# Gate's and up's shared low-rank products together in two folds of the second phase of an fp32 attention and expert-FFN layer

## The chip, the cores and the metric

The kernel runs on one core of a Trainium2 chip. The metric is the device time of one execution in microseconds, the median of several runs. Everything is float32.

## The reference, cut to what matters

```python
xn = layernorm(x)                                   # x: 2 x 1024 tokens, 512 wide
x + attention(xn) + ffn(xn)
# attention: Q, K = elu(.) + 1 of the projections, 16 heads of 32
#   out = (Q @ (K^T V)) / (Q . sum(K) + 1e-8);  out @ wo.T + bo
# ffn (DFF 1376, 8 experts, top 2, rank 8)
gate = x @ W_gate + (x @ sA_gate @ sB_gate) * scale + expert_lora(x, A_gate, B_gate, w)
up   = x @ W_up   + (x @ sA_up   @ sB_up)   * scale + expert_lora(x, A_up,   B_up,   w)
hidden = silu(gate) * up
out  = hidden @ W_down + (hidden @ sA_down @ sB_down) * scale + expert_lora(hidden, ...)
```

The terms with `sA` and `sB` are shared by all tokens. So the kernel adds the product `sA @ sB * scale` to the weights themselves, once, before it uses them. This is called a *fold*. Gate and up each have one: for ten blocks of 128 columns of DFF, taken in pairs `j` and `j + 5` (`NP` is 5), and for the last 96 columns, the *rest*.

## The kernel before, in words

One program works through four phases. The order of the instructions on TensorE (PE), VectorE (DVE), ScalarE (ACT) and GpSimd (POOL) is the order in which the Python code issues them. The transfers on SyncE's queue (SP) are put in order by the scheduler of the language when the program is built. An engine takes its instructions strictly in order, so one that waits holds all behind it.

*Phase one* (to about 178 us) normalises and transposes x, projects the keys, and builds for each of two batches of 1024 tokens the matrix K^T V Wo. The object `Finish` does this last part; for the second batch its products take PSUM banks in turn from four tags `pg0` to `pg3` (`Finish.bank`, L502 to L507). Its last four products (`pko`, L553) are copied out by ACT (L554), and `query_unit(0)` runs around them. Then the pool of eight equal banks `ps` is opened (L996), which hands out banks in rotation. Its first users are the five products `psa` of `shared_factors` (L560): they bring the shared factor sA into `sat`, with rows 0 to 7 of each group of 32 partitions holding one 128-column piece.

*Phase two* (178 to 243 us) computes the queries of the second batch in `query_unit(1, ...)`, a row of products named P2, P1, P6, P5, P7, P3, P4 with hooks between them, then the low-rank inputs `low_rank_in` (L851), the denominators (L873), and the rest columns of gate and up in `rest(0)` and `rest(1)` (L1074 to L1094), which call `between[0]` and `between[1]` after their two halves. Folds in this phase:

- `fold_rest(i)`, with `i` 0 for gate and 1 for up: four matmuls with 8 rows each, one for each piece of 128 rows of the weights, into four banks of their own (L1046), then eight additions on DVE (L1049). Gate's stands in hook P7, up's stands after P4 and `load_last`.
- `fold(0, i)`: `fold_pe` has four such matmuls of 256 columns into four banks (L958), `fold_adds` four additions on DVE (L967), `fold_sums` four sums of weight blocks on DVE (L971 to L974) that the fast 2x2 block products need. Gate's stands in `rest(0)`, up's in `rest(1)`; each bank of 512 columns is half used.

`rest(1)`'s second `between` forms the inner weight sums for products 1, 5 and 6 (L1176 to L1179) on DVE. In between, `attend(1, g)` multiplies the queries with the reciprocal denominators that PE spreads into `pb` (L895, L903), `token_diffs(1, ...)` runs on POOL (L1005), and `token_sums_1` on DVE (L1154 to L1157). After `rest(1)` POOL forms more weight and token sums (L1176 to L1179, L1132, L1154 to L1157).

`load_weights(j, late)` loads the weights of a pair. With `late` it first writes one element of each target on DVE (`hold`, L147), so that the transfer can't start before DVE has come to that place. Pair 0 is loaded so, pair 1 is not.

*Phase three* (243 to about 451 us) has ten units, `unit(j, b)`, with gate and up of one pair for one batch: two levels of 2x2 block products (L1202 and L1262), and low-rank products (L1257). The folds of the pairs 1 to 4 stand in its hooks (`next_pair`). A unit adds its products on DVE (L1284 and others). *Phase four* multiplies the hidden features and the attention with their output weights.

Of the kernel before, what the change touches and what calls it, by code (L numbers as in the profile page):

```python
# [15 lines left out]
P = 128  # L16
# [21 lines left out]
def layer_kernel(  # L38
# [23 lines left out]
    nc = tc.nc  # L62
# [10 lines left out]
    RANK = LR // (E + 1)  # L73
# [4 lines left out]
    NC = D // P  # L78
# [163 lines left out]
    def bank(name, shape=None, tag=None):  # L242
        tag = tag or (next(tags) if tags else "ps")
        return ps_pool[0].tile(shape or [P, TB], F32, tag=tag, name=name)
# [250 lines left out]
    class Finish:  # L495


        def __init__(self, b, pg, ksum):
            self.b, self.pg, self.ksum = b, pg, ksum
            self.made = 0  # L500

        def bank(self, name, shape=None):  # L502
            if self.b == 0:
# [195 lines left out]
    def load_weights(t, w):  # L699
        hold(t[:, 0, 0:1])  # L700
        nc.sync.dma_start(out=t, in_=by_chunk(w))
# [185 lines left out]
    def attend(b, g=None):  # L887

        if b:
            todo = [(c, g) for c in range(NC)]  # L890
            by = []
            for c in range(NC):
                rows = slice(c * 32, (c + 1) * 32)
                by.append(bank(f"pb{b}_{g}_{c}"))
                nc.tensor.matmul(by[c], spread[rows, g, :], dens[b][rows, :], start=True, stop=True)  # L895
        else:
            k = len(attended)
            attended.extend((k, k + 1))
            todo = [(i % NC, i // NC) for i in attended[-2:]]
            by = [bcs[i] for i in attended[-2:]]  # L900
        for (c, g), t in zip(todo, by):
            v = qt[b, c, g]
            nc.vector.tensor_mul(v, v, t)  # L903
            if b == 0:
                spread_den()

            j, i = c % NPQ, c // NPQ
            nc.sync.dma_start(
                out=q_dram[b][j][:, :, 2 * i + g, :].rearrange("s p n -> p s n"),
                in_=v.rearrange("p (s n) -> p s n", n=UT),  # L910
            )
# [35 lines left out]
                )  # L947
        wsum[j] = (ws, sb)

    def fold_pe(j, i, tags=()):  # L950

        sb = wsum[j][1]
        pf = []
        for k in range(NC):
            rows = slice(k * 32, k * 32 + RANK)
            name = f"pf{i}_{j}_{k}"
            pf.append(spare_bank(tags[k], name) if tags else bank(name))
            nc.tensor.matmul(pf[k][:, 0 : 2 * P], sat[rows, i, :], sb[rows, i, :, :], start=True, stop=True)  # L958
        return pf

    def fold_adds(j, i, pf):

        t = wsum[j][0][i]
        v = t.rearrange("p s (k m) -> p s k m", m=P)
        for k in range(NC):
            at = v[:, k // 2 : k // 2 + 7 : 6, k % 2, :]
            nc.vector.tensor_add(at, at, pf[k][:, 0 : 2 * P].rearrange("p (h m) -> p h m", h=2))  # L967

    def fold_sums(j, i):
        t = wsum[j][0][i]  # L970
        nc.vector.tensor_add(t[:, S1, :], t[:, A21, :], t[:, A22, :])  # L971
        nc.vector.tensor_sub(t[:, S3, :], t[:, A11, :], t[:, A21, :])
        nc.vector.tensor_sub(t[:, S2, :], t[:, S1, :], t[:, A11, :])
        nc.vector.tensor_sub(t[:, S4, :], t[:, A12, :], t[:, S2, :])  # L974
# [28 lines left out]
    def token_diffs(b, tag):  # L1003
        xdiff.append(ffn.tile([P, TB], F32, tag=tag, name=f"xdiff{b}"))
        nc.gpsimd.tensor_sub(xdiff[b], xa[b][:, 0:TB], xa[b][:, TB:BT])  # L1005

    def fold(j, i):
        def f():
            fold_adds(j, i, fold_pe(j, i))
            fold_sums(j, i)  # L1010

        return f

    RA = P // 2
# [2 lines left out]
    def rest_cols(i):  # L1019

        return slice(i * RA, (i + 1) * RA), slice(P + i * RB, P + (i + 1) * RB)
# [15 lines left out]
                nc.sync.dma_start(out=sb[k * 32 : k * 32 + RANK, i, :], in_=bw[ER:LR, RC])  # L1037
        return t, sb, bd

    def fold_rest(i):  # L1040
        t, sb, _ = w_rest
        pf = []
        for k in range(NC):
            rows = slice(k * 32, k * 32 + RANK)
            pf.append(bank(f"pfr{i}_{k}"))
            nc.tensor.matmul(pf[k][:, 0:REST], sat[rows, i, :], sb[rows, i, :], start=True, stop=True)  # L1046
        for k in range(NC):
            for at, f in zip(rest_cols(i), (slice(0, RA), slice(RA, REST))):
                nc.vector.tensor_add(t[:, k, at], t[:, k, at], pf[k][:, f])  # L1049

    def rest(b, between=(None, None)):
        t, _, bd = w_rest
        spare = [f"qt{k}{g}" for k in range(NC) for g in range(2)]
        blk = [ts(g, TB) for g in range(2)]

        def gated_rows(ps, first, n, g, dst):

            h, v = (
                p2w.tile([P, TB], F32, tag=spare.pop(0), name=f"{n_}{b}_{g}_{dst.start}", bufs=1) for n_ in ("hr", "ur")
            )  # L1060
            gr, ur = slice(first, first + n), slice(first + n, first + 2 * n)
            nc.scalar.activation(h[gr, :], ps[gr, :], AF.Silu)
            nc.scalar.copy(v[gr, :], ps[ur, :])

            def rest_of():
                nc.vector.tensor_mul(h[gr, :], h[gr, :], v[gr, :])
                nc.sync.dma_start(
                    out=r_dram[b][:, dst, g, :].rearrange("s p n -> p s n"),
                    in_=h[gr, :].rearrange("p (s n) -> p s n", n=UT),
                )  # L1070

            later(rest_of)

        ps = bank(f"pr{b}_2")  # L1074
        halves = [ps[2 * RB * g : 2 * RB * (g + 1), :] for g in range(2)]
        for g in range(2):
            nc.tensor.matmul(halves[g], bd[:, P:], xa[b][:, blk[g]], start=True, stop=False, skip_group_check=True)
        for k in range(NC):
            for g in range(2):
                nc.tensor.matmul(  # L1080
                    halves[g], t[:, k, P:], xt(b, k, blk[g]), start=False, stop=(k == NC - 1), skip_group_check=True
                )
        flush()
        for g in range(2):
            gated_rows(ps, 2 * RB * g, RB, g, slice(RA, REST))
        for g in range(2):
            ps = bank(f"pr{b}_{g}")
            nc.tensor.matmul(ps, bd[:, 0:P], xa[b][:, blk[g]], start=True, stop=False)
            for k in range(NC):
                nc.tensor.matmul(ps, t[:, k, 0:P], xt(b, k, blk[g]), start=False, stop=(k == NC - 1))  # L1090
            flush()
            gated_rows(ps, 0, RA, g, slice(0, RA))
            if between[g]:
                between[g]()  # L1094
# [5 lines left out]
    for _ in range(2):  # L1100
# [1 line left out]
    token_diffs(0, "xd")  # L1102
    query_unit(1, {
        "P5": [lambda: attend(0)],
        "P7": [lambda: fold_rest(0), lambda: attend(0)],
        "P3": [lambda: attend(0)],
        "P4": [lambda: attend(0), lambda: load_weights(0, True)],
    })
    load_weights(1)
    def u_tile(name):  # L1110
        return up_.tile([P, TB], F32, tag="u", name=name)

# [37 lines left out]
    def token_sums_1(eng, b):  # L1150

        t = xnT[b][0][:, :, TB:BT].rearrange("p k (h n) -> p k h n", n=TH)
        b11, b21 = tsum[b][1][:, 0], tsum[b][1][:, 1]
        eng.tensor_sub(t[:, 0, 0], b11[:, TH:], b11[:, 0:TH])  # L1154
        eng.tensor_sub(t[:, 0, 1], b21[:, TH:], t[:, 0, 0])
        eng.tensor_sub(t[:, 1, 0], b21[:, TH:], b11[:, TH:])
        eng.tensor_sub(t[:, 1, 1], b21[:, 0:TH], t[:, 0, 1])  # L1157
        inner_tokens(b, (1,), lambda i, k: t[:, k // 2, k % 2])
# [309 lines left out]
        return sb, wdr, bd, *diffs  # L1468

    sb_d, wdr, bd_sb, wdr_diff, bd_diff = load_last()  # L1470
    fold_rest(1)
    low_rank_in(2)
    low_rank_in(3)
    denominators(1)
    list(token_sums_56(nc.vector, 0, slot(6, [2, 4, TH], "ti56_0")))
    rest(0, (fold(0, 0), lambda: attend(1, 0)))
    attend(1, 1)
    token_diffs(1, "den")
    token_sums_1(nc.vector, 0)
    rest(1, (fold(0, 1), lambda: list(inner_weight_sums(nc.vector, 0, (1, 5, 6)))))  # L1480
    flush()
    ps8.close()
    p2_stack.close()
# [37 lines left out]
    def next_pair(j):  # L1521

        pf = {}


        def pe(i):
            return lambda: pf.update({i: fold_pe(j, i, FREE[i])})

        def adds(i):
            return lambda: fold_adds(j, i, pf.pop(i))  # L1530

        def sums(eng, *ps):
            return lambda: list(inner_weight_sums(eng, j, ps))

        last = {}

        def last_sums(n):
            def f():
                g = last.setdefault(0, inner_weight_sums(nc.vector, j, (1, 5, 6)))
                for _ in range(n):  # L1540
                    next(g, None)

            return f

        return (
            {"6c": [pe(0)], "1d": [adds(0)], "6d": [pe(1)], "7": [adds(1)]},
            {"6c": [lambda: fold_sums(j, 0)], "2c": [lambda: fold_sums(j, 1), sums(nc.gpsimd, 3)],
             "3b": [sums(nc.gpsimd, 2), last_sums(2)], "3d": [last_sums(3)]},
        )
# [572 lines left out]
```

## Time and profile before

| what | value |
|---|---|
| runs | 728.38, 729.91 and 730.34 us; median 729.91 us |
| the profiled execution's own time | 730.1 us |
| its span, first to last instruction | 728.3 us |
| mean granted clock of TensorE | 0.999 |
| PE busy | 717.8 us of the span |
| DVE busy | 579.8 us |
| ACT busy, POOL busy | 198.1 us, 143.4 us |
| PE busy from 168 to 182 us | 13.66 of 14 us |
| PE busy from 182 to 243 us | 61.00 of 61 us |
| PE busy from 243 to 304 us | 60.16 of 61 us |

In the profile a matmul in float32 has two records for each instruction: a product that is one line of the code counts twice. "x8" behind a group of the four fold matmuls is four matmuls. Durations of matmuls overlap with those of their neighbours, since they are pipelined; the chain of work, whose pieces follow each other without overlap, gives the time that a group takes from its neighbours.

### The profile page before, as it was taken

How to read it: one execution, taken by the hardware profiler on the slowest of the kernel's cores; microseconds unless marked ns; L12 is line 12 of the kernel's file. 1: busy time of each engine (PE TensorE's matmuls, PEld its weight loads, DVE VectorE, ACT ScalarE, POOL GpSimd, SP SyncE). 2: the span in 40 equal slices, each digit the busy share in tenths (PEclk: the TensorE clock that was granted, in tenths of full speed). 3: DMA queues.
4: the chain of work that ended last, by engine and by line, in shares of the span. 5: the costliest groups of instructions: out<-in, count | busy, mean ns of one | idle time of the engine just before them, and what ended most of it. 6: DMA issues, size and time to landing. Idle time of an engine off the chain costs nothing.

```text
span 728.3 us, 9908 instructions
## 1 busy us (share of the span) xinstructions
PE 717.8 (99%) x3428; PEld 493.1 (68%) x3428; DVE 579.8 (80%) x1330; ACT 198.1 (27%) x438; POOL 143.4 (20%) x176
## 2 busy tenths in 40 slices
PE   8999999999999999999999999999999999999997
PEld 6666676454433566666667667566688899899896
DVE  5788767777587588878878878878988789998874
ACT  3533412454443233333333333333200000000000
POOL 4014011101000770310310310544520100000000
PEclk9999999999999999999999999999999999999999
DMA  4253000313575101211201201333662444523101
GB/s 155 85 157 106 11 1 1 97 32 112 158 212 154 26 5 58 87 32 59 88 29 59 87 30 59 116 126 134 202 195 101 134 158 132 158 87 109 59 16 44
DMA packets 61734, 66.85 MB, mean 92 GB/s; under 512 B 10866, under 2 KB 49522, under 8 KB 61428
## 3 DMA queue, kind: packets, MB, share of 16 engines
q1 hardware_dynamic: 61154, 66.20, 29.0%
q8 instruction: 27, 0.44, 0.3%
q14 instruction: 23, 0.19, 0.1%
q10 hardware_dynamic: 530, 0.02, 0.0%
HBM read 44.11 MB, written 22.09 MB: 91 GB/s over the span
## 4 chain that ended last, share of the span: by engine, by line
PE 83%; DVE 12%; ACT 3%; issue 1%; DMA 0%; DVEq 0%; ACTq 0%
PE ab L1202 16%; PE b L1262 8%; PE po L1899 7%; PE pg L401 5%; PE pya L1771 4%; PE pxa L1771 3%; PE pqu L772 3%; PE pyb L1771 3%; PE ph L1639 3%; PE x L1202 3%; PE pxb L1771 2%; PE pyc L1771 2%; PE pxa L851 2%; PE b L1257 2%; PE pr L1090 2%; PE pye L1771 2%
## 5 line engine op out<-in xcount | busy, mean ns | idle before, releaser
L1262 PE MATMUL b<-t,w 128*128 128x512 f32 x160 | 83.2, 601 | 0.7 <-DVE t L1284 0.7
L401 PE MATMUL pg<-kt,xn 128*128 128x512 f32 x128 | 58.7, 594 | 0.5 <-DVE kt L345 0.5
L1284 POOL TENSOR_TENSOR r<-r,r 128x512 f32<-128x512 f32 x20 | 30.1, 1524 | 84.5 <-DVE t L1284 82.9
L1202 PE MATMUL ab<-ti,wi 128*128 128x256 f32 x180 | 45.4, 379 | 0.0
L1202 PEld LDWEIGHTS ab<-ti,w 128*128 128x128 f32 x140 | 25.1, 189 | 29.4 <-DVE r L1230 8.2
L1284 DVE TENSOR_TENSOR r<-r,r 128x512 f32<-128x512 f32 x60 | 44.9, 788 | 0.0
L1202 PEld LDWEIGHTS ab<-ti,wi 128*128 128x128 f32 x180 | 34.2, 190 | 13.2 <-issue 5.0
L1202 PE MATMUL ab<-ti,w 128*128 128x256 f32 x140 | 41.2, 387 | 0.5 <-DVE r L1230 0.2
L401 PEld LDWEIGHTS pg<-kt,xn 128*128 128x128 f32 x128 | 23.2, 190 | 22.6 <-issue 20.6
L1235 ACT COPY r<-ab 128x256 f32<-128x256 f32 x50 | 18.6, 372 | 71.1 <-PE ab L1202 71.1
L1230 DVE TENSOR_TENSOR r<-r,ab 128x256 f32<-128x256 f32 x50 | 20.8, 417 | 20.2 <-ACT r L1227 19.7
L1262 PEld LDWEIGHTS b<-t,w 128*128 128x128 f32 x160 | 29.2, 190 | 11.3 <-issue 5.9
L1238 DVE TENSOR_TENSOR r<-r,ab 128x256 f32<-128x256 f32 x50 | 20.8, 417 | 15.9 <-ACT r L1235 15.7
L1212 ACT COPY r<-ab 128x256 f32<-128x256 f32 x50 | 18.6, 373 | 48.5 <-PE ab L1202 47.0
L1899 PE MATMUL po<-wd,f 128*128 128x256 f32 x140 | 30.9, 380 | 0.1
L410 POOL TENSOR_TENSOR ksum<-ksum,kt 128x512 f32<-128x512 f32 x12 | 15.8, 1319 | 71.7 <-DVE lg L447 42.3
L1223 ACT COPY r<-ab 128x256 f32<-128x256 f32 x50 | 18.6, 372 | 40.8 <-PE ab L1202 40.8
L1899 PEld LDWEIGHTS po<-wd,f 128*128 128x128 f32 x140 | 26.4, 190 | 4.4 <-issue 0.5
L1202 PE MATMUL ab<-xnT,w 128*128 128x256 f32 x100 | 29.4, 390 | 0.0
L1842 DVE TENSOR_TENSOR f<-f 128x256 f32<-128x256 f32 x84 | 29.3, 416 | 0.1
L1202 PE MATMUL ab<-xnT,wi 128*128 128x256 f32 x100 | 28.1, 379 | 0.0
L1202 PEld LDWEIGHTS ab<-xnT,w 128*128 128x128 f32 x100 | 18.1, 189 | 10.8 <-issue 4.5
(450 smaller groups left out, 1655.7 us busy)
## 6 DMA issues: line engine op xcount, KB each, us to landing
h_dram<-h SPq DMA_DIRECT2D x40, 256.0 KB
f<-h_dram SPq DMA_DIRECT2D x10, 512.0 KB
x_ring<-in_x_dram SPq DMA_DIRECT2D x16, 256.0 KB
q_dram<-qt SPq DMA_DIRECT2D x16, 256.0 KB
xr<-in_x_dram SPq DMA_DIRECT2D x16, 256.0 KB
out_dram<-xr SPq DMA_DIRECT2D x15, 256.0 KB
w<-in_w_up_dram SPq DMA_DIRECT2D x10, 256.0 KB
w<-in_w_gate_dram SPq DMA_DIRECT2D x10, 256.0 KB
```

What stands on the lines that cost most here:

```text
L401: nc.tensor.matmul(pg[m], xns[n][:, ts(m, P)], kt, start=(j == 0), stop=(j == TPBATCH - 1))
L772: nc.tensor.matmul(banks[c], wqs[p][:, k, ts(c, P)], tsum[b][p][:, k, :], start=(start and k == 0), stop=(k == 1), skip_group_check=True,)
L1202: nc.tensor.matmul(out, w, t, start=start, stop=True, skip_group_check=True)
L1212: nc.scalar.copy(self.r[0][:, H0], self.ua)
L1230: nc.vector.tensor_add(self.r[1][:, H1], self.r[1][:, H1], self.lo)
L1238: nc.vector.tensor_add(self.r[1][:, H0], self.r[1][:, H0], self.lo)
L1262: nc.tensor.matmul(pb[m], ws[m][:, A_OF[p], ts(k, P)], tsum[b][p][:, k, :], start=start, stop=True, skip_group_check=True)
L1284: eng.tensor_add(to[m], t[m], v[m])
L1639: nc.tensor.matmul(phs[u][g * ER : (g + 1) * ER, :], a, f[:, g, :], start=(ns[0] == 0 and n == 0), stop=(last and n == len(chunks) - 1), s ...
L1771: nc.tensor.matmul(o, lhsT, rhs, start=first, stop=True, skip_group_check=True)
L1842: op(t[:, at, :], t[:, x_, :], t[:, y, :])
L1899: nc.tensor.matmul(ps[p][:, q, :], lhsT, rhs, start=start, stop=stop, skip_group_check=True)
```

## The change

- `Finish.made` starts at 3 instead of 0: the banks of the second batch's products shift by one tag. The products `pc`, `pr`, `pv`, `pw0`, `pw1` and the four `pko` stood on pg0, 1, 2, 3, 0 and 1, 2, 3, 0; they stand on pg3, 0, 1, 2, 3 and 0, 1, 2, 3.
- `fold_pe` takes a list of parts `ms`. With both parts, gate's four matmuls write the first halves of four banks, and up's four matmuls the second halves. In phase two both are done in `rest(0)`; DVE adds all eight there (`first_fold`). The eight sums of both parts stand after `token_diffs(1, ...)`. `rest(1)`'s first `between` is now the inner weight sums, its second is empty. In phase three the folds stay apart, up's writing the second half of its banks.
- `fold_rest` is called once, where up's was: eight matmuls into four banks, and eight additions, each over gate and up together. The call in hook P7 is gone.
- Pair 1 is loaded with `late`, which adds four small writes on DVE.

```diff
@@ class Finish
-            self.made = 0
+            self.made = NC - 1
@@
-    def fold_pe(j, i, tags=()):
+    def fold_pe(j, tags=(), ms=(0, 1)):
...
         for k in range(NC):
-            rows = slice(k * 32, k * 32 + RANK)
-            name = f"pf{i}_{j}_{k}"
+            name = f"pf{ms[0]}_{j}_{k}"
             pf.append(spare_bank(tags[k], name) if tags else bank(name))
-            nc.tensor.matmul(pf[k][:, 0 : 2 * P], sat[rows, i, :], sb[rows, i, :, :], start=True, stop=True)
+        for i in ms:
+            for k in range(NC):
+                rows = slice(k * 32, k * 32 + RANK)
+                nc.tensor.matmul(pf[k][:, ts(i, 2 * P)], sat[rows, i, :], sb[rows, i, :, :], start=True, stop=True)
         return pf
@@ def fold_adds
-            nc.vector.tensor_add(at, at, pf[k][:, 0 : 2 * P].rearrange("p (h m) -> p h m", h=2))
+            nc.vector.tensor_add(at, at, pf[k][:, ts(i, 2 * P)].rearrange("p (h m) -> p h m", h=2))
@@
-    def fold_rest(i):
+    def fold_rest():
         t, sb, _ = w_rest
-        pf = []
+        pf = [bank(f"pfr{k}", [P, 2, REST]) for k in range(NC)]
+        for i in range(2):
+            for k in range(NC):
+                rows = slice(k * 32, k * 32 + RANK)
+                nc.tensor.matmul(pf[k][:, i, :], sat[rows, i, :], sb[rows, i, :], start=True, stop=True)
         for k in range(NC):
-            rows = slice(k * 32, k * 32 + RANK)
-            pf.append(bank(f"pfr{i}_{k}"))
-            nc.tensor.matmul(pf[k][:, 0:REST], sat[rows, i, :], sb[rows, i, :], start=True, stop=True)
-        for k in range(NC):
-            for at, f in zip(rest_cols(i), (slice(0, RA), slice(RA, REST))):
-                nc.vector.tensor_add(t[:, k, at], t[:, k, at], pf[k][:, f])
+            for at, f in ((slice(0, P), slice(0, RA)), (slice(P, None), slice(RA, REST))):
+                v = t[:, k, at].rearrange("p (i n) -> p i n", i=2)
+                nc.vector.tensor_add(v, v, pf[k][:, :, f])
@@
-        "P7": [lambda: fold_rest(0), lambda: attend(0)],
+        "P7": [lambda: attend(0)],
...
-    load_weights(1)
+    load_weights(1, True)
@@
-    fold_rest(1)
+    fold_rest()
...
-    rest(0, (fold(0, 0), lambda: attend(1, 0)))
+
+    def first_fold():
+        pf = fold_pe(0)
+        for i in range(2):
+            fold_adds(0, i, pf)
+
+    rest(0, (first_fold, lambda: attend(1, 0)))
     attend(1, 1)
     token_diffs(1, "den")
+    for i in range(2):
+        fold_sums(0, i)
     token_sums_1(nc.vector, 0)
-    rest(1, (fold(0, 1), lambda: list(inner_weight_sums(nc.vector, 0, (1, 5, 6)))))
+    rest(1, (lambda: list(inner_weight_sums(nc.vector, 0, (1, 5, 6))), None))
@@ def next_pair
-            return lambda: pf.update({i: fold_pe(j, i, FREE[i])})
+            return lambda: pf.update({i: fold_pe(j, FREE[i], (i,))})
```

In the built program the counts on PE, ACT and POOL are as before; DVE has eight additions less and four small writes more. On SP's queue four things move: the two loads of up's pair 1, which stood before the first `bc` loads, and those of gate's pair 1 now all follow the loads of pair 0; the small loads for the last phase (`wdr`, `bd_sb`) stand earlier; and the eight small loads `sb2` stand before the eight stores `q_dram1` of `attend(1, ...)` instead of after them.

More of the change, by code (lines that the diff above doesn't have):

```diff
@@ L1005, in token_diffs @@
         nc.gpsimd.tensor_sub(xdiff[b], xa[b][:, 0:TB], xa[b][:, TB:BT])
[L1007 to L1012, printed above, removed]
     RA = P // 2
```

## The prediction

> **What bounds the kernel now.** I read the page first: its busy times, and the shares of the chain of work that ended last.
>
> ```profile
> PE 717.8 (99%) x3428; PEld 493.1 (68%) x3428; DVE 579.8 (80%) x1330; ACT 198.1 (27%) x438; POOL 143.4 (20%) x176
> PE 83%; DVE 12%; ACT 3%; issue 1%; DMA 0%; DVEq 0%; ACTq 0%
> ```
>
> PE is busy for nearly the whole span, and most of the chain is PE's. So what is to be gained is PE time, or one of PE's few waits. The list of waits of PE, asked from 165 to 262 us, where the change lies, has two lines (total us, times, longest):
>
> ```profile
> PE b L1262 <- DVE t L1284: 0.7, 1, 0.7
> PE psa L560 <- ACT gt L554: 0.3, 1, 0.3
> ```
>
> All else in this stretch is PE after PE. The chain of waits shows what the folds take from their neighbours (start, us, what):
>
> ```profile
> 168.34 1.38 PE psa L560 x10
> ...
> 195.81 0.41 PE pfr L1046 x8
> 196.22 3.63 PE pqu L772 x8
> 199.85 3.43 PE pqv L772 x8
> 203.28 0.41 PE pfr L1046 x8
> ...
> 221.54 0.64 PE pf L958 x8
> 222.18 1.06 PE pr L1088 x2
> ...
> 238.01 0.64 PE pf L958 x8
> 238.66 1.06 PE pr L1088 x2
> ```
>
> Eight records of 512 columns take 3.43 us, but 3.63 behind `pfr`; two take 1.06 behind `pf` where 3.43 / 4 = 0.86 is due. So each group of fold matmuls costs its own piece and a restart of 0.20 us in the next. DVE's and POOL's timelines show the rest (start, us, engine, what):
>
> ```profile
> 222.20 1.41 DVE L967 TENSOR_TENSOR w<-w,pf 128x256 f32<-128x256 f32 x4 [1.26 <-PE pf L958]
> ...
> 227.76 4.87 DVE L903 TENSOR_TENSOR qt<-qt,pb 128x512 f32<-128x512 f32 x8 [1.96 <-PE pb L895]
> ...
> 242.19 0.80 DVE L1176 TENSOR_TENSOR wi<-w 128x384 f32<-128x384 f32 x1
> ...
> 256.52 3.35 DVE L1284 TENSOR_TENSOR r<-r,r 128x512 f32<-128x512 f32 x2
> ```
>
> ```profile
> 241.75 0.83 POOL L1176 TENSOR_TENSOR w<-w 128x128 f32<-128x128 f32 x1 [11.31 <-DVE w L974]
> ...
> 257.60 1.72 POOL L1132 TENSOR_TENSOR ti<-t 128x512 f32<-128x512 f32 x1
> ```
>
> DVE has idle time around the folds. POOL starts its sums when the last fold sum is done (L974). The two additions at 256.52 take 3.35 us, where two of this size otherwise take 1.28; they delay the addition that PE waits for at 260.12.
>
> **What the Trainium skill says.** "TensorEngine Tiling (Array Packing)", Key Properties: a change of the tiling mode drains TensorE. The trace agrees: the restart of 0.20 us stands at each change between the 8-row matmuls and full ones. "TensorE: Matmul & The Clock Gate", The mechanism: a weight load runs beside matmuls only where its row group differs. The trace fits: the four row groups run together, so that a group is two waves (a record per row group each), and a wave takes 0.64 / 2 = 0.32 us where 256 columns stream in 0.43 / 2 = 0.21. "SBUF — State Buffer", Who interferes with whom: a DVE instruction with two SBUF inputs and a GpSimd instruction that reads SBUF block each other. The trace agrees: 1.7 us instead of 0.64 at 256.52, beside POOL.
>
> **The change part by part.**
>
> *Shifted banks.* The list of waits has `psa` (bank of pg0) waiting for ACT's copy of `pko`. Before, the last of four copies stood in that bank; now the first does. The four copies take 2.04 us from 166.25 (ACT's timeline), so the first is done by 166.8, and PE comes at 168.0. The idle 0.35 us before `psa` goes, and its first record no longer lasts 377 ns against 275 of the others (`psa`'s instructions): 0.35 to 0.45 us, taken as 0.40. Next late is the bank of the fifth `psa`, which DVE reads from 168.03 to 168.72 (L831); PE gets there at about 168.0 + 8 × 0.11 = 168.9. The bank of the fourth copy now goes to `pxa`, which starts at 169.2; that copy ends at 168.29. Both ends: 0 if another wait takes its place, 0.5.
>
> *`fold_rest` once.* Gone in P7: 0.41 + 0.20 = 0.61 us. Added after P4: two waves, at most another 0.41 us, at least the streaming of 2 × 96 columns, 0.16. Saved 0.20 to 0.45 on PE; I take 0.20, since the same row groups need their weights again. On DVE, P7 loses 1.00 us. After P4 eight additions of 128 and 64 columns replace eight of 64 and 32. From 0.125 us (8 in 1.00, 48 columns on average) and 0.35 us (4 of 256 in 1.41), about 1.1 ns a column: 4 × (0.21 + 0.14) = 1.4 us for 1.0. Cover: PE needs the first result for L1080, at 213.45 before and 212.8 now; DVE, at this place at 210.99 before, has the first piece at 211.5 and the last at 212.5, needed at 215.4. Without that 1.3 us of cover each us late would cost one.
>
> *Both parts of pair 0 in one fold.* `rest(0)` gets two waves more, at most 0.64, at least 2 × 0.21 = 0.43 us; `rest(1)` loses 0.64 + 0.20. Saved 0.20 to 0.41; I take 0.20. DVE's additions wait for the bank's last writer, so they start at about 222.2 as before, since PE has gained 0.6 and spends 0.64. Eight take 2.8 us, to 225.0. The banks go to `pb`, needed from 226.6: 1.6 us of cover. Up's weights must now have landed at 223.6 instead of 238.7: in the DMA view from 211 to 220 us the traffic falls off at the end, with part of pair 1 in it. The fold sums, 2 × 1.47 us, now follow L903 (232.6 to 235.6), so the token sums, the `hr` products and their stores come up to 3 us later, for which only ACT's tiles wait, at 242. The inner weight sums run at about 239 to 242.4, instead of 242.19 to 245.18; PE uses them at 245.57 before. A slack of 0.4 becomes 2.
>
> *Earlier POOL.* Its sums can start at 235.6 instead of 241.75, but the fifth instruction writes over a tile of the `hr` stores, out at about 241.5. Then 21 us of work as before end near 262.5 instead of 266.5. The two DVE additions at 255.7 still lie beside it. I take the wait of 0.7 us as unchanged; ends: all of it gone, or as much again.
>
> *`late` for pair 1.* Four writes of 0.06 us or less on DVE, in the cover named. They wait for slot 8, last read by P3's product on PE (done at 199.8), and hold SP at a place where pair 0's own `late` already held it. The 1 MB now comes after pair 0's; it is needed at 250. SP's queue: `sb2` ahead of the `q_dram1` stores waits for PE's fold (222.2) and is issued by 227, at 0.3 us each, before the first store is ready. Cost nothing; if that cover is gone, see the third rival.
>
> Sum: 0.40 + 0.20 + 0.20 = 0.80 us, from the profiled execution's 730.1 to 729.3. That execution is 0.2 above the median of 729.91, so on the median's footing 729.1 us.
>
> **The rivals.** *First, POOL's earlier end frees DVE.* If POOL doesn't wait at its fifth instruction, it ends near 259, the second addition at 258 runs alone, and PE's wait of 0.7 goes: 728.4 us. For it: POOL's wait was not visible before. Against: the store must land first. *Second, nothing arrives.* The 0.8 us are given back at the first place where DVE, not PE, sets the pace (260.12), because DVE's chain there comes from POOL and not from PE: 729.9 us. For it: that POOL's end, near 262.5, hardly moves with PE. Against: DVE starts that chain at PE's own fold of pair 1. *Third, slower: the stores come late.* The inner weight sums write over `q_dram1`'s source tile. Before, the DMA view from 228 to 242 us falls to almost nothing at 237.8, these stores in. With `sb2` ahead of them, a landing after 242.3 makes PE wait for the third sum (three of 0.8 us, due at 244.7), and each us more costs one. One store's issue took 1.43 us instead of 0.45; at 0.9 us more for each of eight they land 7.2 us later, at 245.0: 729.1 + 2.7 = 731.8 us. Against: `sb2` is small and early.
>
> **How the numbers follow.** Forecast 55% (729.1), first rival 17% (728.4), second 18% (729.9), third and its like 10% (731.8). About 0.3% (2.2 us) is what a measurement of this kernel can tell from no change. All cases but the far ends lie within it: with the upper ends (0.5 + 0.45 + 0.41 + 0.7 = 2.1) and scatter of the runs (1.5 below, 0.4 above the median) faster has 14%, slower 7%, the same 79%. The range takes the upper ends and some scatter below, the second rival with scatter and part of the third above: 727.5 to 730.8 us.
>
> **What would show it.** Right: no wait of PE at `psa`; one `pfr` piece of about 0.8 us and one of `pf` in `rest(0)` of about 1.3 in the chain; one restart each; the wait at 260 shifted but there. Wrong: `pf` pieces under 1.1 us, a new wait of PE at `pb`, at L1080's or at the third L1202 product, or POOL done by 259.

## The result, and the profile after

| | before | changed |
|---|---|---|
| median, 20 runs each | 729.26 us | 727.93 us |
| lowest and highest | 726.82 to 730.58 us | 724.83 to 728.42 us |
| ratio, 95% interval | | 0.9978 [0.9968, 0.9987] |
| profiled execution, own time | 730.1 us | 728.37 us |
| its span | 728.3 us | 726.6 us |

The changed kernel is 1.3 us faster by the medians and 1.7 us by the profiled executions. The run times of most kernels here fall in three groups 1.2 to 1.8 us apart, and one and the same product at 20 us starts up to 3.8 us apart in the profiles of kernels that are the same up to there; so parts of a microsecond are read below from PE's records (good to about 0.02 us), each kernel's start of a product less the same product's start in the kernel before, and not from medians.

The page first, the two lines that were shown of before:

```profile
PE 717.3 (99%) x3428; PEld 493.7 (68%) x3428; DVE 579.0 (80%) x1326; ACT 198.4 (27%) x438; POOL 142.9 (20%) x176
PE 84%; DVE 13%; ACT 2%; issue 1%; DMA 0%; DVEq 0%; ACTq 0%
```

PE still is the bound. The list of PE's waits from 165 to 262 us, which had two lines, is empty: the one at `psa` and the one at 260 us are both gone. In the chain of waits (start, us, what) the folds stand so:

```profile
168.20 1.27 PE psa L560 x10
...
195.55 3.43 PE pqu L772 x8
198.99 3.43 PE pqv L772 x8
202.42 0.63 PE pfr L1041 x16
...
220.90 1.08 PE pf L960 x16
221.97 1.05 PE pr L1084 x2
...
237.80 0.86 PE pr L1084 x2
...
253.47 0.68 PE pf L960 x8
254.15 1.39 DVE w L969 x4
255.55 0.55 DVE r L1281
```

`pqu` takes 3.43 us where it took 3.63 behind `pfr`, and `pr` at 237.80 takes 0.86 instead of 1.06: the restarts went with the folds. But the joined pieces are shorter than I had reckoned: 0.63 us for 16 records of `pfr` against 0.41 for 8, and 1.08 for `pf` against 0.64. DVE and POOL (timelines: start, us, engine, what, idle time before it):

```profile
227.55 4.87 DVE L903 TENSOR_TENSOR qt<-qt,pb 128x512 f32<-128x512 f32 x8 [2.23 <-PE pb L895]
...
255.47 2.67 DVE L1281 TENSOR_TENSOR r<-r,r 128x512 f32<-128x512 f32 x2
```

```profile
235.43 0.57 POOL L1173 TENSOR_TENSOR w<-w 128x128 f32<-128x128 f32 x1 [5.19 <-DVE w L976]
...
241.50 0.58 POOL L1173 TENSOR_TENSOR wi<-w 128x128 f32<-128x128 f32 x1 [3.71 <-DVE wi L1175]
...
254.64 1.27 POOL L1129 TENSOR_TENSOR ti<-t 128x512 f32<-128x512 f32 x1
255.87 1.72 POOL L1129 TENSOR_TENSOR ti<-t,ti 128x512 f32<-128x512 f32 x1
...
261.81 1.28 POOL L1129 TENSOR_TENSOR ti<-xnT,ti 128x512 f32<-128x512 f32 x1
```

POOL starts its sums at 235.4, stands from 237.8 to 241.50 and ends at 263.1, all nearly as forecast (235.6, 241.5, 262.5). DVE's two additions, however, take 2.67 us where they took 3.35.

Set against the kernel before, record by record, PE's starts move like this from 20 us on (they are 0.21 us late there, from the first 14 us):

| place in the kernel before | what | shift of PE there |
|---|---|---|
| 168 to 170 us | `psa` no longer waits | -0.47 us |
| 196 to 197 us | `pfr` of gate gone from P7 | -0.60 us |
| 204 us | the joined `pfr`, one part more | +0.22 us |
| 222 us | the joined `pf`, one part more | +0.43 us |
| 239 us | `pf` of up gone from `rest(1)` | -0.84 us |
| 260.9 us | PE's wait for DVE gone | -0.68 us |
| sum | | -1.94 us |

After 261 us nothing moves to the end of the kernel. -1.94 + 0.21 is the 1.73 us between the two profiled executions.

### The profile page after: what moved, and what is told of

It reads as the page before. It is cut to its first block, busy times and chain, and to the rows that moved or that the text cites. A ratio compares the mean times of both kernels' runs of the same rounds, so it can differ in the third digit from the quotient of the medians.

```text
span 726.6 us, 9905 instructions
## 1 busy us (share of the span) xinstructions
PE 717.3 (99%) x3428; PEld 493.7 (68%) x3428; DVE 579.0 (80%) x1326; ACT 198.4 (27%) x438; POOL 142.9 (20%) x176
## 4 chain that ended last, share of the span: by engine, by line
PE 84%; DVE 13%; ACT 2%; issue 1%; DMA 0%; DVEq 0%; ACTq 0%
PE ab L1199 15%; PE b L1259 8%; PE po L1904 7%; PE pg L401 5%; PE pqu L772 4%; PE pya L1776 4%; PE pxa L1776 3%; PE pyb L1776 3%; PE ph L1644 3%; PE x L1199 2%; PE pxb L1776 2%; PE pyc L1776 2%; PE pxa L851 2%; PE b L1254 2%; PE pqv L772 2%; PE pr L1086 2%
## 5 line engine op out<-in xcount | busy, mean ns | idle before, releaser
L1199 PEld LDWEIGHTS ab<-ti,wi 128*128 128x128 f32 x180 | 34.2, 190 | 13.2 <-issue 4.8
L1281 DVE TENSOR_TENSOR r<-r,r 128x512 f32<-128x512 f32 x60 | 43.1, 758 | 0.0
```

Of the source, the lines that this page charges most:

```text
L1199: nc.tensor.matmul(out, w, t, start=start, stop=True, skip_group_check=True)
L1281: eng.tensor_add(to[m], t[m], v[m])
```

## The experiments

Each kernel is compared with runs of the kernel before on the same chip. The last column is the shift of PE's starts from 20 to 262 us against the profile of before.

| kernel | median us | ratio to before, 95% interval | PE's shift |
|---|---|---|---|
| banks_only | 727.94 | 0.9991 [0.9978, 1.0005] | -0.45 us |
| pair_once | 727.45 | 0.9986 [0.9972, 1.0000] | -1.07 us |
| rest_once | 741.04 | 1.0173 [1.0149, 1.0197] | slower |
| not_late | 739.90 | 1.0153 [1.0129, 1.0176] | slower |
| gate_late | 726.55 | 0.9974 [0.9963, 0.9985] | -1.92 us |
| up_late | 739.86 | 1.0153 [1.0131, 1.0175] | slower |
| rest_late | 729.72 | 1.0002 [0.9991, 1.0013] | -0.34 us |
| late_only | 729.29 | 1.0004 [0.9994, 1.0015] | +0.25 us |
| pool_half | 728.01 | 0.9989 [0.9979, 0.9999] | -1.25 us |
| pool_full | 726.65 | 0.9978 [0.9968, 0.9988] | -1.94 us |
| all_once | 725.71 | 0.9957 [0.9938, 0.9975] | -2.46 us, -3.50 at 430 us |

**The parts alone.** The first set puts each part of the change into the kernel before, or takes one out of the changed kernel.

banks_only:

```diff
-            self.made = 0
+            self.made = NC - 1
```

> The kernel before with the shifted banks alone. If the wait at psa is what the shift removes, the profile has no wait of PE there, all of PE's later work starts 0.45 to 0.5 us earlier, and PE's wait of 0.7 us at 260 us stays: 0.5 us faster. If the gain at 260 us hangs on how DVE and GpSimd happen to alternate there, the wait can also go here, for PE and DVE have moved against GpSimd by nothing: 0.5 us too. If the shift does nothing, 0.

PE has lost its wait at `psa` and 0.45 us, and nothing else moved. The wait at 260 us stays, at 0.8 us:

```profile
PE b L1262 <- DVE t L1284: 0.8, 1, 0.8
```

pair_once, the joint fold of pair 0 and the moved sums:

```diff
-    rest(0, (fold(0, 0), lambda: attend(1, 0)))
+    rest(0, (first_fold, lambda: attend(1, 0)))
...
+    for i in range(2):
+        fold_sums(0, i)
     token_sums_1(nc.vector, 0)
-    rest(1, (fold(0, 1), lambda: list(inner_weight_sums(nc.vector, 0, (1, 5, 6)))))
+    rest(1, (lambda: list(inner_weight_sums(nc.vector, 0, (1, 5, 6))), None))
```

> The kernel before with both parts of pair 0 folded together, the sums moved and the inner weight sums in rest(1)'s first place. By the profile after: PE 0.43 us later behind the joint fold, 0.84 earlier behind rest(1)'s first half, so 0.41 gained. If GpSimd's earlier start is what shortens DVE's two additions at 256 us, PE's wait there goes here too and the gain is 1.1 us. If that was a chance of how DVE and GpSimd alternate, it need not: 0.4 to 1.1.

PE's shifts are +0.43 at 222 us, -0.84 at 239 us and -0.70 at 260.9 us, those of the changed kernel. So 0.41 us come from the fold itself, and the vanished wait at 260 us belongs to this part.

rest_once, the rest columns' products once, without the hold on pair 1's loads:

```diff
-        "P7": [lambda: fold_rest(0), lambda: attend(0)],
+        "P7": [lambda: attend(0)],
...
-    fold_rest(1)
+    fold_rest()
```

> The kernel before with fold_rest called once, up's place. By the profile after, the two added waves cost 0.22 us and the removed group 0.60: PE starts 0.38 us earlier from 204 us on. By my prediction's value it would be 0.20. The wait at 260 us stays at 0.7 by both.

Here theory and rival both missed: 12.5 us slower, 1.7%. not_late, the changed kernel without the hold, came with it:

```diff
-    load_weights(1, True)
+    load_weights(1)
```

> The changed kernel with pair 1 loaded as before, without the writes on DVE that hold the loads. If these are free, as I forecast, the time is that of the changed kernel, 0.99780 of the kernel before, within 0.1%. If the later loads of pair 1 helped (the bc loads and the small loads for the last phase come earlier), it is slower than the changed kernel by some tenths of a us.

It too is 12 us slower than the changed kernel. The list of waits of not_late from 180 to 215 us, and that of SP's queue from 150 to 260 us (total us, times, longest):

```profile
DVE qt L903 <- DMA bc<-d_dram: 17.5, 4, 13.8
...
PE pqv L772 <- DVE qt L819: 9.5, 1, 9.5
```

```profile
SPq L935 <- PE pqu L772: 17.2, 1, 17.2
```

PE waits for DVE, DVE for the loads `bc` of the broadcast denominators, and SP stands 17.2 us at L935, a load of pair 1's weights. SP's timeline of not_late shows what is queued behind it:

```profile
177.98 0.36 SPq L881 DMA_DIRECT2D d_dram<-den  x1
195.61 0.94 SPq L935 DMA_DIRECT2D w<-in_w_gate_dram  x2
196.64 0.46 SPq L935 DMA_DIRECT2D w<-in_w_up_dram  x1
197.19 1.84 SPq L865 DMA_DIRECT2D bc<-d_dram  x4
```

And of the changed kernel:

```profile
181.47 0.35 SPq L881 DMA_DIRECT2D d_dram<-den  x1
181.92 0.37 SPq L1458 DMA_DIRECT2D wdr<-in_w_down_dram  x1
...
183.56 11.06 SPq L865 DMA_DIRECT2D bc<-d_dram  x16
```

And of the kernel before:

```profile
181.68 0.99 SPq L935 DMA_DIRECT2D w<-in_w_up_dram  x2
...
183.36 11.52 SPq L865 DMA_DIRECT2D bc<-d_dram  x16
...
210.91 0.42 SPq L935 DMA_DIRECT2D w<-in_w_gate_dram  x1
```

Gate's load of pair 1 writes slot 8, which in not_late PE's last `pqu` product reads until 195.6 us. There the load was put ahead of `bc`; in the kernel before, where the first `fold_rest` still stood in P7, the same load had been put behind seven of the eight stores `q_dram0`, and only up's load, whose tile was free, stood ahead of `bc`.

PE's wait is not all that is lost. PE's timeline of rest_once at the products behind the wait, and of the kernel before at the same products:

```profile
205.11 6.56 PE L772 MATMUL pqv<-t,wq_sb 128*128 128x512 f32 x8 [8.89 <-DVE qt L819]
```

```profile
199.69 3.60 PE L772 MATMUL pqv<-t,wq_sb 128*128 128x512 f32 x8
```

The same eight records take 3.0 us longer. In rest_once's trace the granted clock of TensorE is 0.50 from 200.7 to 210.9 us, and 1.00 before and after. From 20 us to the end PE's starts move by +11.6 us in rest_once: -0.60 for the group gone from P7, +9.06 at the first record behind the wait, +2.96 over the eight records, +0.22 for the joined `pfr`, and next to nothing after that.

**Which load.** If that is all, holding gate's load alone must be enough, and holding up's alone must not help.

gate_late (for up_late, `i == 1`):

```diff
-                if late:
+                if late and (j == 0 or i == 0):
```

> The changed kernel, but of pair 1's weights only gate's load (slot 8) is held back, up's is not. Theory (head of SP's queue): in the two slow kernels SP stood 17.2 us at the load of w0_1, gate's weights of pair 1, whose slot is read until the last product of unit 1's queries with the weight sums (pqu, 195.6 us); the loads of the broadcast denominators (bc) stand behind it in SP's order, and DVE, then PE, wait for these. Up's load w1_1 has nothing to wait for. So holding gate's alone is enough: built, its load stands behind batch 0's stores, and up's ahead of bc; 727.9 within 0.3%, no wait of PE at pqv, bc loads begin within 1 us of where they begin in the changed kernel. Rival (both loads, or the bytes that they move at that time, slow the path to bc): part of the 12 us stays, 731 to 740.

> The changed kernel, but of pair 1's weights only up's load is held back, gate's is not. Theory (head of SP's queue): gate's load stands ahead of the bc loads in SP's order and waits for the same product as before, some 17 us; DVE waits 13 to 14 us for bc, PE about 9 us at pqv: 739.9 within 0.3%. Rival (the bytes moved at that time): only half of them are left, 731 to 737. Rival (it is up's load): 727.9.

Both came out as the theory had it, 0.9974 against 1.0153, and the runs leave neither rival: with up's loads ahead of it, gate_late issues the first `bc` at 181.57 us, 2.0 us sooner than the changed kernel in absolute time and level with it once the different start of the two profiles (1.9 us) is taken off. up_late's waits, of SP's queue from 176 to 205 us and of PE from 165 to 262 us:

```profile
SPq L935 <- PE pqu L772: 17.0, 1, 17.0
```

```profile
PE pqv L772 <- DVE qt L819: 8.5, 1, 8.5
```

SP and PE stand as in not_late, though only half of the held bytes were let go.

rest_late, rest_once with the hold, and late_only, the hold alone in the kernel before:

```diff
-    load_weights(1)
+    load_weights(1, True)
```

> The kernel before with two parts of the change: the rest columns' products once, and pair 1's loads held back. Theory (the slowness of the kernel with the first alone is gate's load at the head of SP's queue and nothing else): no wait of PE at pqv, 0.38 us less on PE than the kernel before, the wait at 260 us stays at 0.7 to 0.8: 0.4 us faster, 0.9995. Rival (doing the products once costs by itself, through later additions on DVE): 731 to 740.

> The kernel before with pair 1's loads held back and nothing else. Theory (the hold is free by itself, since before no load of pair 1 stood ahead of the bc loads that had to wait): 728.5, the ratio within 0.2% of 1, the wait at 260 us stays. Rival (the hold is worth something or costs by itself): off by 0.3% or more.

With the hold, rest_once is no longer slow. PE's shift (-0.36 us at 210 us, -0.34 at 262 us) is the size of this part; by the ratio alone no difference can be told. late_only's ratio is 1 within its interval. Its profile has 0.2 us lost at 210.7 us, where the fourth `pd` product of a group went off 0.2 us after the other three; neither the changed kernel nor rest_late has that. DVE's last two products L903 start 0.9 us later there than in the kernel before (210.67 against 209.75 us). Whether that comes from the hold, through the changed order on SP's queue, is not shown.

**The wait at 260 us.** The change didn't free DVE of POOL, and yet the two additions became shorter. In the kernel before, the first came at 256.52 us, 0.14 us after this POOL instruction had started:

```profile
256.38 1.27 POOL L1132 TENSOR_TENSOR ti<-t,ti 128x512 f32<-128x512 f32 x1
```

In the changed one it came at 255.47, 0.83 us after one (254.64), and finished in 0.99 us instead of 1.68. If the two engines take turns, only where the addition falls within a POOL instruction counts, not when POOL ends. Two kernels put one instruction more into POOL's stream; pool_full takes `[:, :, 0]` on all three views for pool_half's `[:, 0, 0]`:

```diff
     list(token_sums_23(0, slot(4, [2, 4, TH], "ti23_0")))
+    nc.gpsimd.tensor_sub(ti56_1[:, 0, 0], tsum_pair[1][:, 0, 0, TH:TB], tsum_pair[1][:, 0, 0, 0:TH])
     token_sums_1(nc.gpsimd, 1)
```

> The changed kernel with one more instruction on POOL, a 128x256 subtraction (0.68 us from start to start in this kernel) ahead of its token sums; the value is computed again later. Theory (alternation): PE's wait at 260 us went because DVE's first addition of unit (0, 0) at 255.5 us came 0.83 us after the start of a POOL instruction of 1.27 us, and not 0.14 us after one as in the kernel before. Shifted by 0.68 us it comes 0.15 us after one again: the two additions take 3.3 us and not 2.7, and PE's wait of about 0.7 us is back; 728.6. Rival (POOL's end or its load decides): a later end by 0.7 us changes nothing by itself, no wait, 727.9.

> The changed kernel with one more instruction on POOL, a 128x512 subtraction (1.22 us from start to start in this kernel) ahead of its token sums; the value is computed again later. Theory (alternation): POOL's starts around 255.5 us fall where they fell, since its instructions there follow each other at 1.22 us: the two additions take 2.7 us, no wait of PE, 727.9, although POOL ends 1.2 us later. Rival (POOL's end or its load decides): a wait of at least that of the half step, 0.7 us or more, 728.6 to 729.1.

pool_half's list of waits of PE, and DVE's and POOL's timelines:

```profile
PE b L1259 <- DVE t L1281: 0.7, 1, 0.7
```

```profile
251.78 3.35 DVE L1281 TENSOR_TENSOR r<-r,r 128x512 f32<-128x512 f32 x2
```

```profile
251.63 1.27 POOL L1129 TENSOR_TENSOR ti<-t 128x512 f32<-128x512 f32 x1
```

The addition comes 0.15 us after POOL's start, the pair takes 3.35 us to the hundredth as in the kernel before, and PE's wait is back. pool_full gives POOL the larger instruction, and PE has no wait:

```profile
253.62 2.67 DVE L1281 TENSOR_TENSOR r<-r,r 128x512 f32<-128x512 f32 x2
```

```profile
252.79 1.27 POOL L1129 TENSOR_TENSOR ti<-t,ti 128x512 f32<-128x512 f32 x1
```

The addition comes 0.83 us after POOL's start, as in the changed kernel. The larger added instruction cost nothing, the smaller one 0.7 us: it is the place within POOL's instruction that decides, and neither POOL's end nor its load. All 13 profiles agree to the hundredth: the first addition and the second each end 0.55 us after the end of the POOL instruction in which they came.

**The same in the third phase.** If a part that joins a fold costs 0.43 us and a fold of its own 0.84, pairs 1 to 4, which the change leaves apart, have the same to give. all_once:

```diff
-            {"6c": [pe(0)], "1d": [adds(0)], "6d": [pe(1)], "7": [adds(1)]},
+            {"6c": [pe], "1d": [adds(0, 0, 1), adds(1, 0, 1)], "6d": [adds(0, 2, 3)], "7": [adds(1, 2, 3)]},
```

Here `pe` is `fold_pe(j, FREE[0])` with both parts, and `adds(i, *ks)` adds part i for the ks named, so that the banks `held0` and `held1` are free again in time.

> The changed kernel, with gate's and up's products of pairs 1 to 4 together as well: both parts at the hook that gate's had (after the third piece of unit (j, 0)), the additions of k = 0 and 1 of both parts where gate's four were, those of k = 2 and 3 of both where up's were. Theory (an added part costs 0.43 us of streaming, a fold of its own 0.84): four folds of 0.84 us go, four parts of 0.43 come, 1.6 us less than the changed kernel, 726.3 where that has 727.9, 0.9955 of the kernel before. Rival (up's weights, loaded ahead of the unit, are not there yet for the earlier additions, or the banks held longer make PE wait): a new wait of PE behind DVE in each of the four units; nothing gained or slower, 727.9 to 732.

0.9957 [0.9938, 0.9975], the fastest of all. The chain of waits of the changed kernel at pair 2 (start, us, what), and of all_once:

```profile
302.64 0.78 PE pf L960 x8
...
308.12 0.64 PE pf L960 x8
308.76 1.05 PE b L1259 x2
```

```profile
301.85 1.22 PE pf L960 x16
```

PE gains 0.35 us in each of pairs 2 to 4 and 0.5 in pair 1, together 1.55 us more than the changed kernel, where four times 0.41 were expected: an added part costs 0.44 us there and a fold of its own 0.79. PE has no new wait, so up's weights were there.

## Why the prediction was right, and where its terms were off

The forecast of 729.1 us lies 1.2 us above the measured median of 727.93, which is inside the range, 0.43 us above its lower edge. Of the 1.2 us, 0.65 lie in the footing: the median of the kernel before was 729.91 us in three runs and 729.26 in twenty. The wait at `psa` and the restarts that were to go did go. The reason given for the price of an added part was wrong, and so was the forecast that the wait at 260 us stays. All four terms came out near their upper ends, 1.94 us in sum against 2.1, and the range was made to take these in. The largest of them, 0.68 us, stood in the prediction only as an end and as its first rival: that it came is luck.

*Shifted banks.* Taken as 0.40 us, measured 0.47 in the changed kernel and 0.45 alone. Next late was nothing, as worked out.

*`fold_rest` once.* Taken as 0.20 us "since the same row groups need their weights again", measured 0.38. The step that failed is that reason: I charged the added waves for their weight loads. The instruction records of the joined `pf` show otherwise. Its four waves start at 220.83, 221.15, 221.37 and 221.58 us: the second comes 0.32 us after the first, the third and fourth each 0.22, which is the streaming of 256 columns alone. A weight load of the second wave runs from 220.94 to 221.12 us, beneath the first wave, and one of the third from 221.15 to 221.34, beneath the second, in the same row groups. So the 0.1 us more behind the first wave need not be a reload: behind a fold, the first full product shows it too, 0.53 us to the next one instead of 0.43. That it is the first wave's own load, which has no wave before it to run beneath, fits but is not shown. The waves of `pfr` stand 0.19, 0.11 and 0.11 us apart. So an added part of `pf` costs the lower bound that I had written down, 0.43 us. An added part of `pfr` costs 0.22 us where the bound was 0.16; why its waves don't follow at the 0.08 us of their streaming stays open.

*Both parts of pair 0.* For the same reason 0.41 us instead of 0.20, the upper end of what I gave. DVE's cover held: no wait of PE at `pb`. My own sign that something was wrong, "`pf` pieces under 1.1 us", came (1.08).

The Trainium skill ("TensorE: Matmul & The Clock Gate", The mechanism) has a weight load run beside matmuls only where its row group differs. With all four row groups busy the trace doesn't agree, from the second wave of a fold on, and the measurement decides. The same section also lets PE take a load ahead when it goes to a background weight buffer, a case that the prediction left out; no run here shows whether that is what happens. What the prediction drew from the page was wrong: 0.32 us, half of a fold of two waves, is not the price of an added wave.

*Earlier POOL.* POOL did what was forecast, and the wait, which I took as unchanged with "all of it gone" as an end, was all gone: 0.68 us. The first rival gave 728.4 us for this, the profiled execution's time, but its reason (POOL done near 259) was false: POOL waited at its fifth instruction as I said, and ended at 263.1. That POOL lay beside the additions still was right; that the wait would therefore stay was not, since it depends on the place within one POOL instruction, which no step of mine worked out.

*`late` for pair 1.* "Cost nothing" holds in the changed kernel as far as the traces tell: PE has no wait there, and gate_late, with two of the four writes, gains 1.92 us against 1.94. But it was the wrong question: I asked what the hold costs and not what stands ahead of whom without it. The hold of gate's load is what makes the single `fold_rest` possible (banks_only and pair_once do without it); in the kernels that have the single `fold_rest` without it (rest_once, not_late, up_late), the order built for SP's queue puts gate's load ahead of `bc`, and they are some 12 us slower. The danger on SP's queue that I did price, `sb2` ahead of the stores `q_dram1`, did not come: no wait of PE there.

The sum: 0.47 + 0.38 + 0.41 + 0.68 = 1.94 us where I had 0.40 + 0.20 + 0.20 + 0 = 0.80, less 0.21 us of the first 14 us, which the change doesn't touch. Why the order built for SP puts gate's load at two so different places is not settled; only the order and its price are.

## What to carry to other kernels

Small matmuls that fill all row groups are cheapest together: each group of them costs some 0.4 us beyond its streaming (0.84 us where 0.43 stream), and a part that joins a group costs its streaming and little more. When an edit removes work, look at what the queue's order becomes, above all at loads into a tile that is still read: one such load at the head of a queue costs all that stands behind it, whatever it carries itself. A wait of one engine behind another's stream of long instructions can come or go with a shift of half an instruction; it is worth a look, and not worth a claim.

## What the hardware showed that I had not expected

- A weight load of 8 rows ran beneath the streaming of the wave before in the same row groups, from the second wave on; the third and fourth waves followed at 0.22 us (256 columns) and 0.11 us (96 columns).
- DVE's addition of 128x512 took 0.98 to 1.00 us when it came 0.82 to 0.84 us after the start of a 1.27 us POOL instruction, 1.16 us at 0.66 us after it, 1.67 to 1.71 us at 0.11 to 0.15 us after it, and 0.68 us with POOL idle (pool_half at 260.57 us). It waits for the end of the one instruction and ends 0.55 us after it; the next addition meets the next POOL instruction and takes 1.75 or 1.76 us in all these cases.
- In the three kernels where PE stood for 8.5 to 9.5 us at `pqv`, the granted clock of TensorE fell to 0.50 for 10.24 us, beginning 3.4 to 4.9 us after PE had stopped. No other profile has such a fall between 20 and 720 us. In rest_once the eight `pqv` records, at 0.85 us from one to the next instead of 0.43, lost 3.0 us to it. So the wait of 8.9 us cost about 12 us.
- A halved pace stands at the start of the kernel too: in the profile of before the products `pk` of 256 columns follow at 0.43 us until 13.2 us and at 0.22 after that, in that of banks_only at 0.22 from 8.4 us on. This is most of the 3.1 us by which the two differ at 20 us.
